# A two-layer gated network on one core: other places for projection steps, transform sums and gate steps in the queues

## The chip, the core and the metric

The kernel runs on one core of a Trainium2 chip. A core has five engines, each with a queue of its own that it works through in order: TensorE (PE; its weight loads are listed as PEld), VectorE (DVE), ScalarE (ACT), GpSimd (POOL) and SyncE (SP, which here only issues DMAs). Semaphores order the engines among each other. The metric is device time in microseconds, from the start to the end of one execution; lower is better. The profile gives the TensorE clock that was granted as a share of full speed: in this case it is 1.00 or 0.50 at any moment.

## The reference

Inputs are x and a context of 8 sequences of 256 tokens by 1024 features, all float32. Two layers follow one another; each adds a gated mixing step and a gated feed-forward step to x.

```
x = x + tanh(g_xattn[0]) * autocorrelation(layernorm(x), ctx, ctx)
x = x + tanh(g_ffn[0])   * lora_ffn(layernorm(x))
x = x + tanh(g_xattn[1]) * attention(layernorm(x), ctx, ctx, mask)
x = x + tanh(g_ffn[1])   * fourier_ffn(layernorm(x))
```

- autocorrelation: correlate x and the context along the sequence by Fourier transforms, per feature; keep the 11 largest lags of each feature, softmax over them, and add up the context shifted by those lags (positions past the end repeat the last token).
- lora_ffn: x W' + b, plus a low-rank product whose rank (8, 16, 32 or 64) the best of four gate scores selects for each token.
- attention: 32 query heads, 8 key and value heads of 128, with rotary positions; keys and values come from the context.
- fourier_ffn: a linear layer plus a low-rank update whose coefficients are masked and passed through a real Fourier basis. It is linear in x, so it can be folded into one matrix.

## The kernel before

**Passes and stages.** The batch is worked in two passes of four sequences. A pass has four stages: `autocorrelation`, `lora_ffn`, `attention`, `fourier_ffn`. x stays in SBUF as eight tiles of 128 rows by 1024 in each pass. The second half of each sequence is stored turned round, so that a transform along the sequence works on sums and differences of the two halves.

**Products by seven.** All large products are made with seven half-size products in place of eight (`SEVEN = (1, 2, 6, 7, 4, 5, 3)` is their order). `left_operands` and `right_operands` make the operands from four sums or differences of quarters. Which engine makes the sums is an argument. `combine` and `add_product` take the seven results out of PSUM.

**Stage 1.** `autocorrelation` runs beside a generator, `keys_values`, that makes the attention's keys and values of all tokens in the pass. One call of `fill(1)` draws one step from it: half of one of the seven products, eight matmuls of 256 columns (L794). A block of 512 tokens has four weight halves (two of keys, two of values) of 14 steps each, so 56 steps, and a pass has two blocks. In pass 0 the generator goes on with `fold_last_layer` (17 steps, L302 and L320), which makes the last stage's matrix and stores it in DRAM. In the first block of pass 0 the weight sums are made on the fly by `made_weight`: those of the keys on VectorE, those of the values (`wv`) on GpSimd, as eight instructions (L154, L158). Each block after the first makes four context sums as eight GpSimd instructions. The weights' loads are queued after the fourth product of the weight half before.

The autocorrelation works on half batches: one sequence by 512 features, eight in a pass. `turn(this, before, coming)` handles three of them at once:

1. for `coming`, it loads the context rows `cn` and the row `end`;
2. for `this`, it transforms the keys' sums (`ke`, `ko`; L412) and the queries' (`qe`, `qo`), copies spectra to SBUF on ACT, and multiplies them (`products`: four VectorE multiplications, then two GpSimd sums, L432 and L434 or L436). The results of the multiplication are `re` and `im`;
3. it transforms the values' half frequencies (`vr`, `vi`);
4. for `coming`, `sums` makes the normed rows `xn` on ACT (L453), then `ke`, `ko`, `qe`, `qo` on GpSimd (L461 to L464), and corrects `ke` on VectorE (L467);
5. for `before`, it transposes the weights of the lags (`both`; L515), transforms them, and multiplies with the keys' and values' spectra: `er`, `ei`, then `odr`, `odi`;
6. for `this`, `correlation` (L561, L562) returns `re` and `im` to lags, in two parts; `lags` finds the largest on VectorE and weighs them; GpSimd forms `both` from the result `w` (L552, L553). Between the parts `back(0)` and `back(1)` return the values of `before` in two matmuls each (L531), and `residual` (L371) adds them to x.

`fill` calls stand between these steps. When no `before` exists (the first half batch), those inside `if before` aren't made; a last turn has only a `before`.

At the start of a pass, `loads(order[0])`, two small tables and `late()` (the loads of six x tiles) are queued on SP, then `fill`, the norm of the first sequence, `sums` of the first half batch and another `fill`.

**Stages 2 and 4.** Both feed-forward stages work on four pairs of row tiles. `prepare` norms a tile, transposes it on PE (L366) and copies it back on ACT as `xnT`, which has two buffers. In `lora_ffn` it also computes the low-rank product and the gate scores (`pa`, L623) and forms the gated low-rank activations `xa` in a chain of small VectorE instructions (L630 to L642). `turned` transposes `xa` on PE (`px`, L647) and copies it on ACT (`xaT`); `neg` is its negative, for the fourth product. `left` makes the pair's operand sums. `project` runs the seven products of the pair before (L670 with L679, and L1123), with the results in four PSUM buffers, and yields after each in `lora_ffn`. The sums of the first pair are made on VectorE, those of the other three on GpSimd (L206 to L209).

**What sets the order.** The text gives each instruction its engine and a rank. The order in the engines' queues is laid out when the program is built and isn't always the order of the text: in the trace, transposes of the next stage stand among the fold's last matmuls. Within a queue the engine waits at the instruction in front.

Of the kernel before, what the change touches and what calls it, by code (L numbers as in the profile page):

```python
# [11 lines left out]
F32 = mybir.dt.float32  # L12
# [3 lines left out]
ALU = mybir.AluOpType  # L16
# [3 lines left out]
P = 128  # L20
# [9 lines left out]
R0 = 64  # L30
# [9 lines left out]
KH = KC // 2  # L40
# [6 lines left out]
def flamingo_kernel(ctx: ExitStack, tc: tile.TileContext, a: dict, out: bass.AP):  # L47
    nc = tc.nc
# [320 lines left out]
    def residual(xs, ps, g):  # L369

        nc.vector.scalar_tensor_tensor(xs, ps, g, xs, ALU.mult, ALU.add)  # L371
# [12 lines left out]
    def autocorrelation(p, xt, pools, beside, late):  # L384
        c1, w1, w2, ps_dft, ps_cor, ps_out = pools

        def fill(n):
            for _ in range(n):
                next(beside, None)
# [59 lines left out]
        def sums(b, cols, cn, end):  # L449

            xn = big_tile("xn", [2, HALF], "xn")
            for i, lin in enumerate(norms[b]):
                nc.scalar.activation(  # L453
                    xn[:, i, :],
                    xt[b * 2 + i][:, cols],
                    AF.Identity,
                    bias=lin[:, 1:2],
                    scale=lin[:, 0:1],
                )
            qe, qo, ke, ko = one("qe"), one("qo"), one("ke"), one("ko")  # L460
# [12 lines left out]
        def turn(this, before, coming):  # L473


            after = None
            if this:
                b, cols, end, qe, qo, ke, ko = this
                if coming:
                    coming = loads(coming)  # L480
                kr_ps, ki_ps = dft((KCE, ke)), dft((KSE, ko), (NYQ, ke))


                kr, ki, kn = sb("kr"), sb("ki"), sb("kn")
                nc.scalar.copy(kr, kr_ps)
                nc.scalar.copy(kn, kr_ps)
                nc.scalar.activation(ki, ki_ps, AF.Copy, scale=pair)
                nc.scalar.copy(kn[0:1, :], ki_ps[0:1, :])
                re, im = sb("re"), sb("im")
                products(spectrum((CE, SE), (qe, qo)), kr, ki, kn, re, im, False)  # L490
                fill(2)

            if this:
                vr_ps, vi_ps = dft((KCO, ko)), dft((KSO, ke))
                vr, vi = sb("vr"), sb("vi")
                nc.scalar.copy(vr, vr_ps)
                nc.scalar.copy(vi, vi_ps)

                nc.vector.scalar_tensor_tensor(
                    kr[0:1, :], end[0:1, :], 2.0 * S, kr[0:1, :], ALU.mult, ALU.add  # L500
                )
                if coming:
                    after = sums(*coming)
                fill(2)
            last = not this
            if before:
                if last:
                    fill(3)
# [12 lines left out]
                fill(2 if last else 1)  # L521
                odr, odi = one("odr"), one("odi")
                products(spectrum((CO, SO), wt[::-1]), bvr, bvi, bvr, odr, odi, True)
                fill(3 if last else 1)

            def back(l):

                if before:
                    po = ps_out.tile([P, HALF], F32, tag="out", name="po")
                    for i, (k, sp) in enumerate(((0, er), (3, odi)) if l == 0 else ((1, ei), (2, odr))):  # L530
                        nc.tensor.matmul(po, inv2[:, k, :], sp, start=(i == 0), stop=(i == 1))  # L531
                    residual(b_tiles[0][:, b_cols], po, tg_x[0])
                    residual(b_tiles[1][:, b_cols], po, ntg_x[0] if l else tg_x[0])
                    fill(1)

            if last:
                back(0)
                back(1)
                return None, None
            w = big_tile("xn", [4, S], "w")  # L540
            cor = correlation(re, im, 0)
            fill(1)
            back(0)
# [48 lines left out]
        nc.sync.dma_start(inv, a["dft_inv"])  # L592
        inv2 = c1.tile([P, 4, P], F32, name="inv2")
        nc.sync.dma_start(inv2, a["lag_inv"])
        late()
        fill(6 if p == 0 else 4)
        normalize(0, 1)
        this, before = sums(*first), None
        fill(7 if p == 0 else 3)
        for i in range(len(order)):  # L600
            this, before = turn(this, before, order[i + 1] if i + 1 < len(order) else None)
            if i == 0:
# [4 lines left out]
    def lora_ffn(xt, w0, make_w0, ag, bl, beside):  # L607

        with (
# [32 lines left out]
                    nc.vector.tensor_scalar(xa[:, r], pa[:, r], past[:, i : i + 1], None, ALU.mult)  # L642
                return xnT, xa

            def turned(xnT, xa):
                px = ps_s.tile([R0 + 1, P], F32, tag="s", name="px")
                nc.tensor.transpose(px, xa, ident)  # L647
                xaT = w2.tile([R0 + 1, P], F32, tag="xaT", name="xaT", bufs=4)
                nc.scalar.copy(xaT, px)
                return xnT, xaT  # L650

            def left(m, first, second):
                q = [[s[0][:, k * KH : (k + 1) * KH, :] for k in range(2)] for s in (first, second)]
                s = [w2.tile([P, KH, P], F32, tag=f"s{i}", name=f"s{i}") for i in (1, 2, 4)]
                ops = left_operands(nc.gpsimd if m else nc.vector, q, *s)
                neg = w2.tile([R0 + 1, P], F32, tag="neg", name="neg")
                nc.vector.tensor_scalar(neg, second[1], -1.0, None, ALU.mult)
                return ops, first[1], second[1], neg

            def project(m, ops, up, low, neg):  # L660
                x = [
# [27 lines left out]
            for m in range(TT // 2):  # L689
                norm = norm_stats(xt[m * 2 : m * 2 + 2])  # L690
                got = [prepare(m * 2 + i, norm) for i in range(2)]
                steps = project(*pending) if pending else iter(())
                for _ in range(2):
                    next(steps, None)
                got = left(m, *(turned(*x) for x in got))
                if pending is None and make_w0:
                    w0.update(make_w0())
                for _ in steps:
                    pass
                pending = (m, *got)  # L700
            beside(w2, ps_t, "t")
            for _ in project(*pending):
                pass
# [382 lines left out]
    def fourier_ffn(p, xt, groups):  # L1086
        with (
# [16 lines left out]
                transposed(xnT, xn, ps_t, "t")  # L1104
                return xnT

            def left(m, first, second):
                q = [[s[:, k * KH : (k + 1) * KH, :] for k in range(2)] for s in (first, second)]
                s = [w2.tile([P, KH, P], F32, tag=f"s{i}", name=f"s{i}") for i in (1, 2, 4)]
                return left_operands(nc.gpsimd if m else nc.vector, q, *s)  # L1110

            def project(m, ops):
                x = [
# [25 lines left out]

            pending = None  # L1140
            for m in range(TT // 2):
                got = left(m, prepare(m * 2), prepare(m * 2 + 1))
                if pending is not None:
                    project(*pending)
                pending = (m, got)
# [207 lines left out]
```

## Time and profile before

Three runs took 3439.76, 3440.97 and 3441.66 us, with 3440.97 as the median. The profiled execution took 3440.27; its span, from the first instruction to the last, is 3438.5.

| what | us |
| --- | --- |
| span | 3438.5 |
| PE busy | 3335.6 |
| DVE busy | 2227.5 |
| POOL busy | 1413.8 |
| ACT busy | 860.5 |
| PE waits longest at L531 for POOL's `odi` (8 times) | 18.1 |
| one step of the generator, L794, 8 matmuls (63.73 to 65.46) | 1.73 |
| GpSimd sum of 128 x 512 (L206, mean) | 1.27 |
| VectorE sum of 128 x 512 (L206, 436.80) | 0.68 |
| granted clock, mean | 0.984 |

Stage by stage in the first pass: the autocorrelation runs to about 403, the first feed-forward stage from there to about 560, attention to 1647 and the last stage to 1757. The second pass follows in the same order and ends at 3438.5.

How to read it: an engine that is busy all the time bounds the kernel; its idle time, and what ended each idle stretch, tell what could be gained. In a list of waits a row names the waiting engine, its tile and line, whom it waited for, the total in microseconds, how often, and the longest. In a timeline a row has the start, the duration, the engine, line, operation, output and inputs; brackets give the idle time just before it and what ended it. Where rows are merged, the number of instructions is given with x.

### The profile page before, as it was taken

The page shows a single profiled execution, that of the slowest core. Times are in us where ns is not written, and L with a number is a line of the kernel's source. Part 1 is how long each engine was busy: PE and PEld are TensorE (multiplying, and loading weights), DVE is VectorE, ACT ScalarE, POOL GpSimd, SP SyncE. Part 2 cuts the span into 40 slices and gives each one's busy share as a digit, 9 for nine tenths or more (in the row PEclk, how much of TensorE's full clock was granted, in tenths as well). Part 3 has the DMA queues.
Part 4 walks back from the last instruction along what each step waited for, and adds up shares of the span by engine and source line. Part 5 has one row for each costly group of instructions (what it writes and reads, how often), then busy time and mean ns, then how long its engine had stood idle before and what let it go on. Part 6 is the DMA issues. An engine that isn't in the chain of part 4 may idle for free. (4 is left out here: it accounts for less than half of the span.)

```text
span 3438.5 us, 36954 instructions
## 1 busy us (share of the span) xinstructions
PE 3335.6 (97%) x12784; PEld 2287.7 (67%) x12784; DVE 2227.5 (65%) x4181; ACT 860.5 (25%) x2061; POOL 1413.8 (41%) x1259
## 2 busy tenths in 40 slices
PE   7899989999999999999999999999999999999998
PEld 6576545877766776776466666477777776776754
DVE  7677555877777666666557675456666666666562
ACT  2232101222222322223123321122222322222220
POOL 3665222343443344344546542323443344344443
PEclk9899889999999999999999999999999999999999
DMA  7343533333333333343153334053333333333411
GB/s 266 117 141 108 189 144 128 127 137 135 135 135 125 121 117 124 119 160 112 62 193 116 135 114 148 0 178 114 119 123 116 117 119 123 120 117 126 156 38 49
DMA packets 161864, 431.72 MB, mean 126 GB/s; under 512 B 21476, under 2 KB 56292, under 8 KB 161678
## 3 DMA queue, kind: packets, MB, share of 16 engines
q1 hardware_dynamic: 160526, 425.17, 36.7%
q0 software_dynamic: 1152, 4.19, 0.3%
q8 instruction: 102, 1.67, 0.2%
q14 instruction: 84, 0.69, 0.1%
HBM read 350.66 MB, written 78.64 MB: 125 GB/s over the span
## 5 line engine op out<-in xcount | busy, mean ns | idle before, releaser
L715 POOL TENSOR_TENSOR qT<-rope,rope 128x512 f32<-128x512 f32 x128 | 170.1, 1329 | 864.9 <-DVE rope L714 864.9
L950 PE MATMUL po<-wo,oT 128*128 128x512 f32 x960 | 432.1, 593 | 0.0
L921 PE MATMUL ps_q<-xn,wq 128*128 128x256 f32 x1920 | 428.9, 379 | 0.0
L371 DVE SCALAR_TENSOR_TENSOR x<-po,tg,x 128x512 f32<-128x512 f32 x376 | 268.8, 745 | 227.1 <-PE po L950 70.6
L921 PEld LDWEIGHTS ps_q<-xn,wq 128*128 128x128 f32 x1920 | 365.0, 190 | 50.3 <-PE po L679 0.5
L983 ACT ACTIVATE s<-s,nmx 128x256 f32<-128x256 f32 x512 | 255.9, 500 | 275.1 <-DVE nmx L980 274.6
L978 DVE COPY_PREDICATED s<-keep,ps_s 128x512 f32<-128x512 uint8 x256 | 186.1, 730 | 182.4 <-PE ps_s L969 178.9
L950 PEld LDWEIGHTS po<-wo,oT 128*128 128x128 f32 x960 | 177.5, 190 | 175.5 <-issue 170.4
L950 PE MATMUL po<-wo,oS 128*128 128x512 f32 x640 | 287.7, 593 | 0.3 <-DVE x L371 0.3
L921 PE MATMUL ps_q<-xn_t,wq 128*128 128x256 f32 x1280 | 285.6, 379 | 0.0
L1010 ACT COPY wT<-pt 128x512 f32<-128x512 f32 x256 | 138.0, 590 | 516.3 <-PE pt L1004 516.3
L921 PEld LDWEIGHTS ps_q<-xn_t,wq 128*128 128x128 f32 x1280 | 243.3, 190 | 33.0
L1015 PE MATMUL av<-wT,v 128*128 128x256 f32 x1024 | 247.7, 385 | 2.9 <-ACT wT L1010 2.9
L969 PE MATMUL ps_s<-kT,qT 128*128 128x256 f32 x1024 | 248.1, 379 | 0.0
L1015 PEld LDWEIGHTS av<-wT,v 128*128 128x128 f32 x1024 | 192.4, 191 | 78.0 <-issue 43.9
L992 DVE TENSOR_SCALAR s<-s,tot 128x256 f32<-128x256 f32 x512 | 219.6, 469 | 7.7
L977 POOL MEMSET s<- 128x512 f32 x256 | 129.9, 527 | 223.0 <-PE pt L1004 221.3
L950 PEld LDWEIGHTS po<-wo,oS 128*128 128x128 f32 x640 | 119.0, 190 | 136.6 <-issue 128.9
L969 PEld LDWEIGHTS ps_s<-kT,qT 128*128 128x128 f32 x1024 | 192.0, 190 | 25.4 <-DVE x L371 0.5
L258 POOL TENSOR_TENSOR x<-x,part 128x512 f32<-128x512 f32 x80 | 114.8, 1435 | 196.4 <-ACT part L257 196.4
L980 DVE TENSOR_REDUCE nmx<-s 128x2 f32<-128x512 f32 x256 | 175.0, 685 | 8.3
L263 POOL TENSOR_TENSOR x<-x,part 128x512 f32<-128x512 f32 x80 | 102.9, 1287 | 166.9 <-DVE part L371 143.7
(259 smaller groups left out, 5643.1 us busy)
## 6 DMA issues: line engine op xcount, KB each, us to landing
wq<-in_wq_dram SPq DMA_DIRECT2D x104, 512.0 KB, 3.3
wo<-in_wo_dram SPq DMA_DIRECT2D x104, 512.0 KB, 3.4
wq<-wq_d SPq DMA_DIRECT2D x96, 512.0 KB, 3.2
wo<-wo_d SPq DMA_DIRECT2D x96, 512.0 KB, 3.2
w<-w_d SPq DMA_DIRECT2D x36, 512.0 KB, 4.5
wk<-in_wk_dram SPq DMA_DIRECT2D x26, 512.0 KB, 5.4
wv<-in_wv_dram SPq DMA_DIRECT2D x26, 512.0 KB, 4.1
wk<-wk_d SPq DMA_DIRECT2D x24, 512.0 KB, 3.8
```

What stands on the lines that cost most here:

```text
L371: nc.vector.scalar_tensor_tensor(xs, ps, g, xs, ALU.mult, ALU.add)
L715: nc.gpsimd.tensor_add(dst, t0, t1)
L921: nc.tensor.matmul(ps[:, l, :], wops[r][:, l, c, :], xo[r][:, c, :], start=(c == 0), stop=(c == KH - 1),)
L950: nc.tensor.matmul(po, ops[r][:, h, t * P : (t + 1) * P], wops[r][:, h, :], start=(h == 0), stop=(h == 1),)
L969: nc.tensor.matmul(ps[:, t, :], qT[i, n][:, l, t * P : (t + 1) * P], kT[:, n * S : (n + 1) * S], start=True, stop=True,)
L977: nc.gpsimd.memset(s, MASKED)
L978: nc.vector.copy_predicated(s, keep[b], ps)
L980: nc.vector.tensor_reduce(nmx, s, AX.X, ALU.max, negate=True)
L983: nc.scalar.activation(s[:, t, :], s[:, t, :], AF.Exp, bias=nmx[:, t : t + 1], accum_out=tot[:, t : t + 1],)
L992: nc.vector.tensor_scalar(s[:, t, :], s[:, t, :], tot[:, t : t + 1], None, ALU.mult)
L1010: nc.scalar.copy(wT[i], pt)
L1015: nc.tensor.matmul(av[:, i, :], kv[step][1][:, n * 2 + c, :], wT[i][:, c, :], start=(c == 0), stop=(c == 1),)
```

## The change

It changes five things.

1. `fill` counts in the autocorrelation. Before the first half batch, pass 0 draws 12 and 9 steps instead of 6 and 7, and pass 1 draws 0 and 7 instead of 4 and 3. The 12 are drawn ahead of `late()`, so the six x loads come behind what these steps queue. Inside a turn, the step count after the values' transforms goes from 2 to 6 in the first turn of pass 0, from 2 to 1 in its later turns, and stays 2 in pass 1. After the second products it goes from 1 to 2. The fill behind `back(1)` goes.
2. `sums(*coming)` is called after the products of `before` instead of ahead of them.
3. The two returns change places: the first takes `ei` and `odr`, the second `er` and `odi`; the signs follow.
4. In `lora_ffn`, `left` comes ahead of `turned`, and `turned` and `neg` come three products later.
5. All operand sums of both feed-forward stages are made on VectorE.

```diff
-                if coming:
-                    after = sums(*coming)
-                fill(2)
+                fill((1 if p == 0 else 2) if before else 6 if p == 0 else 2)
...
                 products(spectrum((CO, SO), wt[::-1]), bvr, bvi, bvr, odr, odi, True)
-                fill(3 if last else 1)
+                fill(3 if last else 2)
+            if this and coming:
+                after = sums(*coming)
...
-                    for i, (k, sp) in enumerate(((0, er), (3, odi)) if l == 0 else ((1, ei), (2, odr))):
+                    for i, (k, sp) in enumerate(((0, er), (3, odi)) if l else ((1, ei), (2, odr))):
                         nc.tensor.matmul(po, inv2[:, k, :], sp, start=(i == 0), stop=(i == 1))
                     residual(b_tiles[0][:, b_cols], po, tg_x[0])
-                    residual(b_tiles[1][:, b_cols], po, ntg_x[0] if l else tg_x[0])
-                    fill(1)
+                    residual(b_tiles[1][:, b_cols], po, tg_x[0] if l else ntg_x[0])
+                    fill(1 - l)
...
+        if p == 0:
+            fill(12)
         late()
-        fill(6 if p == 0 else 4)
         normalize(0, 1)
         this, before = sums(*first), None
-        fill(7 if p == 0 else 3)
+        fill(9 if p == 0 else 7)
...
-                got = left(m, *(turned(*x) for x in got))
+                ops = left(*(x[0] for x in got))
                 if pending is None and make_w0:
                     w0.update(make_w0())
+                for _ in range(3):
+                    next(steps, None)
+                up, low = (turned(x[1]) for x in got)
+                neg = w2.tile([R0 + 1, P], F32, tag="neg", name="neg")
+                nc.vector.tensor_scalar(neg, low, -1.0, None, ALU.mult)
                 for _ in steps:
                     pass
-                pending = (m, *got)
+                pending = m, ops, up, low, neg
...
-                return left_operands(nc.gpsimd if m else nc.vector, q, *s)
+                return left_operands(nc.vector, q, *s)
```

More of the change, by code (lines that the diff above doesn't have):

```diff
@@ L643, in prepare, with turned @@
                 return xnT, xa
-            def turned(xnT, xa):
+            def turned(xa):
                 px = ps_s.tile([R0 + 1, P], F32, tag="s", name="px")
@@ L649, in turned, with left @@
                 nc.scalar.copy(xaT, px)
-                return xnT, xaT
-            def left(m, first, second):
-                q = [[s[0][:, k * KH : (k + 1) * KH, :] for k in range(2)] for s in (first, second)]
+                return xaT
+            def left(first, second):
+                q = [[s[:, k * KH : (k + 1) * KH, :] for k in range(2)] for s in (first, second)]
                 s = [w2.tile([P, KH, P], F32, tag=f"s{i}", name=f"s{i}") for i in (1, 2, 4)]
[L655 to L658, printed above, removed]
+                return left_operands(nc.vector, q, *s)
             def project(m, ops, up, low, neg):
@@ L1105, in prepare, with left @@
                 return xnT
-            def left(m, first, second):
+            def left(first, second):
                 q = [[s[:, k * KH : (k + 1) * KH, :] for k in range(2)] for s in (first, second)]
                 s = [w2.tile([P, KH, P], F32, tag=f"s{i}", name=f"s{i}") for i in (1, 2, 4)]
-                return left_operands(nc.gpsimd if m else nc.vector, q, *s)
+                return left_operands(nc.vector, q, *s)
             def project(m, ops):
@@ L1141, in fourier_ffn @@
             for m in range(TT // 2):
-                got = left(m, prepare(m * 2), prepare(m * 2 + 1))
+                got = left(prepare(m * 2), prepare(m * 2 + 1))
                 if pending is not None:
```

## The prediction

> **What bounds the kernel now.** First the busy times and the clock row of the page:
>
> ```profile
> PE 3335.6 (97%) x12784; PEld 2287.7 (67%) x12784; DVE 2227.5 (65%) x4181; ACT 860.5 (25%) x2061; POOL 1413.8 (41%) x1259
> ...
> PEclk9899889999999999999999999999999999999999
> ```
>
> PE is busy for 97% of the span, and the change removes no matmul. So it can win only what PE idles (3438.5 - 3335.6 = 103 us, 5.9 of it before the first matmul and 9 behind the last) and what matmuls lose at half clock. Second, the waits of PE alone (total, times, longest):
>
> ```profile
> PE po L531 <- POOL odi L434: 18.1, 8, 5.4
> PE po L531 <- POOL re L432: 11.7, 4, 9.2
> PE px L647 <- DVE xa L642: 10.4, 6, 1.7
> ...
> PE ps_cor L561 <- POOL re L432: 5.7, 1, 5.7
> ...
> PE ps_cor L562 <- POOL im L436: 2.9, 1, 2.9
> ```
>
> These 48.8 us stand at places that the diff touches: L531 is the values' return, L561/L562 the correlation, px the turned gates. Third, stretches in time (us, busy time of PE, PEld, DVE, ACT, POOL, granted clock, DMA):
>
> ```profile
> 47.80:58.00 10.20, 6.30 (x14) 4.59 (x15) 9.77 (x15) 0.30 (x1) 9.67 (x7) 0.50 0.23 73
> 99.00:119.50 20.50, 8.21 (x15) 4.73 (x16) 16.80 (x37) 1.45 (x4) 13.37 (x10) 0.50 0.20 78
> 157.00:160.40 3.40, 3.40 (x8) 2.08 (x7) 1.74 (x3) 0.00 (x0) 3.28 (x3) 0.50 0.14 46
> ...
> 1942.20:1952.40 10.20, 7.83 (x14) 3.96 (x13) 8.08 (x24) 1.41 (x3) 5.04 (x4) 0.50 0.19 59
> ```
>
> Behind a wait the granted clock is 0.50, so half of the PE time in such a stretch is lost besides the wait. Fourth, what POOL does before the longest wait (PE stands from 96.7 to 105.9):
>
> ```profile
> 90.06 2.49 POOL L154 TENSOR_TENSOR wv_s<-wv,wv 128x512 f32<-128x512 f32 x2
> 92.52 2.48 POOL L158 TENSOR_TENSOR wv<-wv,wv 128x512 f32<-128x512 f32 x2
> ...
> 104.58 1.27 POOL L432 TENSOR_TENSOR re<-ma,mb 128x512 f32<-128x512 f32 x1
> ...
> 111.61 1.71 POOL L434 TENSOR_TENSOR odi<-ma,mb 128x512 f32<-128x512 f32 x1
> ```
>
> The values' weight sums (eight of about 1.24, 10 us) lie ahead of the parts that PE awaits, and u and c behind them hold DVE's rope, which idles 12.1 us. Fifth, the gates while POOL forms the next pair's sums:
>
> ```profile
> 476.29 1.94 DVE L634 TENSOR_TENSOR sc<-sc 128x1 f32<-128x1 f32 x2
> ...
> 478.26 1.31 DVE L636 TENSOR_SCALAR past<-sc,best 128x3 f32<-128x3 f32 x1
> ...
> 480.28 0.29 PE L647 MATMUL px<-ident,xa 128*65 128x128 f32 x1 [1.73 <-DVE xa L642]
> ```
>
> With POOL silent, one L634 takes 0.15 and L636 0.23 (497.5 to 499.1).
>
> **The change, part by part.** One call of the keys' and values' generator is eight matmuls, 1.73 us of PE.
>
> (a) More calls ahead. Pass 0 has drawn 14 when its first half batch starts and 20 at that turn's end; afterwards 22 and 32. Pass 1 keeps 8, with the norm queued ahead of them. In pass 0 the correlation's waits (5.68 + 2.89 = 8.57) lie at 43 to 53, when DVE and POOL make the products. The calls that should fill them need the second key weights, issued from 33.3 to 39.2 and landing 8.6 to 10.9 later, with DMA at 0.9 and more of its time. The six loads of x (3 MB, 7 us at 410 GB/s) are put behind these calls' DMAs: a store of k, four of weights, four loads, two stores of k, whose last is out at 43.9. If SP keeps that order, the weights land up to 7 us sooner; x lands by about 44 + 6 + 8 = 58, and the second half batch's cn goes out at 50 instead of 44. Their readers are the third half batch's xn (ACT, 79.1) and the second's transforms (68.9): 11 us or more hide both, and past that a late load costs its lateness. I take 6 of the 8.57 and 1 of the half clock's 3.15 (6.30 / 2): 7 us; bounds 0 (weights late) and 11.7.
>
> (b) The values' weight sums are made in call 29, which moves from the second turn into the first, where no values' return waits on POOL. Their waits, 9.24 + 5.39 = 14.63, and 8.21 / 2 = 4.1 of clock go. Late next is the second half batch's ke and ko, behind 10 us of sums: 10 + 2 x 1.27 against four calls and two correlations of PE work (6.9 + 3.5 = 10.4), 2 us, and with u and c in between 5; with its clock I charge 7.7. That leaves 11 of 18.7; bounds 0 and 18.7.
>
> (c) Values' parts and next sums. The first return now takes ei and odr instead of er and odi: odr is out 1.25 before odi. One more call stands ahead of it (1.73): 2.98 more slack. The waits there are 2.09 and 0.39 + 2.56 in pass 0, and 1.40, 1.58, 0.70 + 1.67, 1.36 + 2.58, 0.85 in pass 1: 15.2 us, of which 2.98 leaves only 0.96. The next half batch's four sums (4 x 1.27 on POOL, two 0.76 on ACT, one 0.68 on DVE) no longer come ahead of er to odi. Half clock behind those waits: 3.4 / 2 twice, 7.83 / 2, 3.4 / 2: 9.0. The stretch at 1942 also follows a 1.9 us wait for DVE that stays. I take 14.2 + 5.3 = 19.5; bounds 8 (a third) and 24.2.
>
> The Trainium skill (TensorE: Matmul & The Clock Gate, "Why this matters for your kernels") says that idle gaps up to about 3 us don't bring the half clock back. The stretch at 157.0 follows a wait of 2.09 and has 0.50, so here the measurement decides. By the rule this part would give 14.2 instead of 19.5.
>
> (d) Sums queued later. The cost is on the next turn's first transform. In the turn at 206 to 244 odi ends at 232.1; four sums after it end at 237.2, ke's DVE step at 238; the transform starts at 243.8: 6 us of slack. In the turns where POOL also makes the context's sums (eight, 10 us) 4 us are missing; that is one turn in each pass, with half of it in clock. Charge 4; bounds 0 and 14 (1 us in each of 14 turns).
>
> (e) Gates and sums of the first FFN. Six waits of 1.73. Their cause is DVE slowed beside POOL's L206 to L209, which go to DVE (4 x 0.68 instead of 4 x 1.27); the turn is asked three products later (10 us). The second gate can't come sooner, since its tile is written only when the pair before has read the buffer, in its fifth product. neg waits on DVE for ACT's 0.26 us copy of the turned gates, with evictions 3.4 us apart behind it, so it holds no one. I take 10; bounds 0 (DVE sums queued into the chain keep it as late) and 10.4.
>
> (f) Sums on VectorE in both FFNs: 12 groups of 2.7 us, or 7 where POOL runs beside them (L154 on DVE took 1.77 at 52.9 instead of 0.68). Behind them in the queue stand the evictions that free PSUM for PE. The cover is a pair's PE time, 34.9 and 25.8 us with DVE about half busy, and four PSUM buffers of 3.4 each. Cost 0; without cover 12 x 2.7 = 33.
>
> (g) Four calls of the fold move into the last turn. The stretch from 409.6 to 447.1 at 0.50 (37.1 busy) stays: 0, bounds -5 and +5.
>
> Sum: 7 + 11 + 19.5 - 4 + 10 = 43.5. The profiled execution took 3440.3, 1.8 around its span of 3438.5; 3440.3 - 43.5 = 3396.8. The median of the runs is 0.7 higher, so 3397.5, rounded to **3397**.
>
> **Rivals.**
>
> 1. *The POOL waits change places.* (a) and (b) together give 4 and (d) takes 8: 4 + 19.5 - 8 + 10 = 25.5, 3416. For it: POOL's work stays the same, only its order moves. Against: the first turn has no return for it to delay.
>
> 2. *All of it goes*: 11.7 + 18.7 + 24.2 + 10.4 = 65 and none of (d): 3376. For it: the queues have slack in most turns (no wait from 180 to 270). Against: 10 us blocks remain on POOL.
>
> 3. *Slower: the next sums land behind this half batch's "both".* POOL waits there for ACT's w (102.3 us in 14 waits, 15.6 the longest). At 213.0 both is done; sums behind it would end ke and ko at 215.5 and DVE at 216.2, against a transform at 205.9: 10.3 a turn. It decides from five of the 14 turns on (43.5 / 10.3); in eight it is 82 - 43.5, 3480. For it: sums now stand directly ahead of both. Against: their inputs are loaded a turn's length before.
>
> 4. *Short waits don't lower the clock*, and the half-rate stretches behind waits under 3 us stay: 5.3 less, 3402. For it: the wait of 3.02 at 306 is followed by full clock; against, 157.0. This is the Trainium skill's rule above.
>
> 5. *The change doesn't do what it says*, since queue order isn't text order: the fold's masks are loaded at 80.8, 300 us before their use, and the next stage's transposes run among the fold's matmuls. Then x keeps its place, the calls fill as before, and (c)'s swap and (e) remain: 8 + 10, 3423.
>
> **How the numbers follow.** Forecast 0.42; rivals 0.20, 0.15, 0.08, 0.06, 0.09. What a measurement can tell from no change is 0.2%, 7 us: 3434 to 3448. Faster holds all but rival 3 and the ends of 1 and 5: 0.86; same 0.05; slower 0.09. The range runs from 3373, under rival 2, to 3432, over rival 5, and leaves out rival 3 and the far ends of (d) and (f). The forecast's own range is 3385 to 3408.
>
> **What would show it.** (a): no wait at L561/L562 before 60 us. (b): L154/L158 of wv run on POOL before the first "both", and no wait over 6 us in 60 to 120. (c): L531 waits under 4 us in all, and now for odr. (d): waits of L412 on ke or qe. (e): no px wait, and L634 at 0.15. (f): no wait of L670 or L1123 for DVE evictions. I am wrong if L412 shows more than 20 us of waits, or if PE's idle time falls by less than 20.

## The result and the profile after

The changed kernel takes 3409.8 us (median of six executions, 3400.7 to 3412.6), beside 3440.4 for the kernel before (3438.8 to 3445.2). The ratio is 0.9907, with a 95% interval from 0.9894 to 0.9919. So it is 30.6 us faster; the forecast was 3397 with a range from 3373 to 3432. The median lies in the range, 13 us above the forecast and just outside the narrower range, 3385 to 3408, that the prediction gave for its main line.

The profiled execution is the fastest of the six: 3400.7, span 3399.0. Where half-clock stretches fall differs from one execution to the next, so a single profile of this kernel may be 9 us from its median.

In the lines of the changed kernel, L531 has become L532, L561/L562 are L562/L563, L647 is L649, L634/L636 are L636/L638 and L794 is L798; L428 to L467 keep their numbers. From its page, the busy times and the clock:

```profile
PE 3319.6 (98%) x12784; PEld 2281.0 (67%) x12784; DVE 2245.2 (66%) x4229; ACT 859.5 (25%) x2061; POOL 1355.3 (40%) x1211
...
PEclk9999899999999999999999999999999999999999
```

The number of matmuls is the same. What PE does not work is 3399.0 - 3319.6 = 79.4 us, 23.5 less than the 102.9 before; its busy time is 16.0 less; the mean granted clock is 0.989 instead of 0.984. Together that is the 39.5 between the two profiled spans. The kernel turn_early below has the same instructions in the same order, and its profile (3409.2) lies near the median: there PE is without work for 26.1 us less than before and busy for 5.0 less, 31.1 together. So by that profile the greater part of what was won is waits, and little of it is clock.

The waits of PE in the changed kernel (total, times, longest) at the places that the prediction named:

```profile
PE po L532 <- DVE x L371: 5.9, 4, 4.0
...
PE dft L412 <- DVE ke L467: 5.4, 1, 5.4
...
PE po L532 <- POOL odr L432: 3.9, 1, 3.9
...
PE po L532 <- DVE neg L576: 3.7, 1, 3.7
...
PE ps_k L798 <- DVE wk_s L158: 3.4, 1, 3.4
PE po L532 <- POOL im L434: 2.0, 2, 1.2
...
PE px L649 <- DVE xa L644: 0.8, 1, 0.8
```

The waits of the correlation (8.6 us) are gone, and so are the two long ones of the return behind the values' weight sums (14.6) and nearly all of px (10.4). But the other waits at the return, 15.2 us before, are 15.5 now (5.9 + 3.9 + 3.7 + 2.0; 13.6 in turn_early), only with other releasers. That is the term that failed.

Two waits that the prediction did not name are gone as well. These are rows of the kernel before, where PE waits for weights of the first FFN and for VectorE's sum of them:

```profile
452.36 3.70 PE L670 MATMUL po<-w,xnT 128*128 128x512 f32 x8 [3.60 <-DMA w<-in_w_dram]
...
462.56 3.70 PE L670 MATMUL po<-w_t,s 128*128 128x512 f32 x8 [2.89 <-DVE w_t L140]
```

Together they are 6.5 us. In the kernel before, six of these eight loads are issued between 446 and 450, after the first product has begun at 443; in the changed kernel all eight are issued between 417 and 423, and the first product begins at 425.

The stretches that correspond to those of the prediction, by time (PE, PEld, DVE, ACT, POOL, granted clock, DMA):

```profile
44.00:54.00 10.00, 6.63 (x32) 5.54 (x31) 9.91 (x15) 0.00 (x0) 2.24 (x2) 1.00 0.91 334
84.00:104.50 20.50, 15.14 (x48) 9.28 (x47) 18.36 (x54) 9.06 (x17) 11.10 (x8) 0.83 0.65 195
...
1947.00:1966.00 19.00, 13.66 (x37) 7.70 (x37) 17.34 (x41) 5.69 (x11) 7.55 (x7) 0.82 0.34 105
```

The first had 0.50 and now 1.00. The second had 8.21 of PE work in 20.5 us at 0.50, now 15.14 at 0.83. The third, in the second pass, still has a lowered clock. From the timeline, the values' weight sums and what follows them:

```profile
73.12 2.94 POOL L154 TENSOR_TENSOR wv_s<-wv,wv 128x512 f32<-128x512 f32 x2
76.02 3.39 POOL L158 TENSOR_TENSOR wv<-wv,wv 128x512 f32<-128x512 f32 x2
...
86.42 1.70 POOL L461 TENSOR_TENSOR ke<-cn 128x512 f32<-128x512 f32 x1
```

```profile
89.94 2.08 PE L412 MATMUL dft<-ke,mats 128*128 128x512 f32 x2 [5.36 <-DVE ke L467]
```

They run 17 us earlier than before (at 73 instead of 90), ahead of the first "both", and POOL comes to ke only behind them: the transform waits 5.36 for it. Last, the gates of the first FFN, for the second tile of the second pair:

```profile
451.18 0.15 DVE L636 TENSOR_TENSOR sc<-sc 128x1 f32<-128x1 f32 x1
...
452.58 0.22 DVE L638 TENSOR_SCALAR past<-sc,best 128x3 f32<-128x3 f32 x1
```

One step on a column takes 0.15 again, where two took 1.94 beside POOL.

### The profile page after: what moved, and what is told of

Read it like the earlier page. It is cut to its first block, busy times and chain, and to the rows that moved or that the text cites. A ratio compares the mean times of both kernels' runs of the same rounds, so it can differ in the third digit from the quotient of the medians.

```text
span 3399.0 us, 36938 instructions
## 1 busy us (share of the span) xinstructions
PE 3319.6 (98%) x12784; PEld 2281.0 (67%) x12784; DVE 2245.2 (66%) x4229; ACT 859.5 (25%) x2061; POOL 1355.3 (40%) x1211
## 5 line engine op out<-in xcount | busy, mean ns | idle before, releaser
L371 DVE SCALAR_TENSOR_TENSOR x<-po,tg,x 128x512 f32<-128x512 f32 x376 | 269.0, 745 | 201.3 <-PE po L954 70.6
L258 POOL TENSOR_TENSOR x<-x,part 128x512 f32<-128x512 f32 x80 | 114.9, 1436 | 213.5 <-ACT part L257 193.6
L716 DVE TENSOR_TENSOR rope<-c,tab_q 128x512 f32<-128x512 f32 x128 | 88.4, 691 | 125.8 <-POOL c L240 119.9
```

## The experiments

Each experiment stands with what was expected of it before it ran; A and B are the two theories of that text. There are twelve kernels, in the order in which they follow here. The times are medians (fastest to slowest), each with its ratio to the kernel before on the same chip (3442 to 3443 there).

| run | what differs from the changed kernel | us | ratio, 95% interval |
|---|---|---|---|
| turn_early | gates turned three products earlier | 3410.2 (3405.2 to 3411.2) | 0.9900 (0.9885 to 0.9915) |
| pool_sums | FFN sums on GpSimd again | 3421.3 (3419.5 to 3423.8) | 0.9937 (0.9923 to 0.9950) |
| x_loads_first | x loads ahead of the 12 steps | 3412.5 (3405.3 to 3415.0) | 0.9906 (0.9893 to 0.9920) |
| fills_only | numbers of calls and place of x loads alone | 3426.3 (3420.0 to 3428.5) | 0.9954 (0.9940 to 0.9967) |
| sums_early | next sums at their old place | 3415.3 (3413.8 to 3421.7) | 0.9922 (0.9908 to 0.9935) |
| returns_old | values' parts in their old places | 3409.3 (3408.1 to 3410.0) | 0.9904 (0.9889 to 0.9920) |
| two_out_banks | returns 2 banks, transforms 3 | 3434.0 (3432.3 to 3436.4) | 0.9973 (0.9962 to 0.9984) |
| second_return_own_bank | second return in a transforms' bank | 3416.2 (3414.6 to 3417.5) | 0.9924 (0.9910 to 0.9937) |
| sums_behind_returns | next sums behind both returns | 3406.5 (3402.1 to 3410.4) | 0.9898 (0.9882 to 0.9915) |
| q_sums_on_vector | qe, qo on VectorE | 3405.7 (3403.9 to 3411.9) | 0.9896 (0.9880 to 0.9913) |
| call_sums_on_vector | u, c of a call on VectorE | 3395.6 (3391.8 to 3398.0) | 0.9861 (0.9846 to 0.9877) |
| call_sums_and_ke_on_vector | u, c and ke on VectorE | 3381.0 (3376.5 to 3387.0) | 0.9816 (0.9802 to 0.9829) |

### The gates: later turn, or sums on VectorE?

turn_early takes the three products out again:

```diff
-                for _ in range(3):
-                    next(steps, None)
                 up, low = (turned(x[1]) for x in got)
```

> The changed kernel, with the turned gates asked three products earlier again; the sums stay on VectorE. Theory A (the px waits came from VectorE's gate chain running slowly beside GpSimd's sums, so taking these sums off GpSimd removed them): px waits stay under 2 us in all, time as the changed kernel, 3400 to 3413. Theory B (asking three products later removed them): six waits of about 1.7 us come back, 10 us more, about 3420.

pool_sums puts the sums of pairs 2 to 4 back on GpSimd and leaves the later turn:

```diff
-            def left(first, second):
+            def left(m, first, second):
...
-                return left_operands(nc.vector, q, *s)
+                return left_operands(nc.gpsimd if m else nc.vector, q, *s)
...
-                ops = left(*(x[0] for x in got))
+                ops = left(m, *(x[0] for x in got))
```

The last stage gets the same edit.

> The changed kernel, with the operand sums of pairs 2 to 4 in both feed-forward stages on GpSimd again; the gates stay late. Theory A (port shared by VectorE and GpSimd slows the gate chain): six px waits of 1.7 us come back, L636 near 1 us instead of 0.15, 10 us slower than the changed kernel, about 3419. Theory B (the later turn removed the waits): px waits stay under 2 us, time within 3 us of the changed kernel.

The first measured 3410.2, and the order of the instructions on every engine is that of the changed kernel: where the turn stands in the text changes nothing in the queues. So it is also a second set of executions of the changed kernel. The second measured 3421.3, and its waits of PE show px again (seven waits, 10.9 us):

```profile
PE px L649 <- DVE xa L644: 10.9, 7, 1.7
```

Both are as theory A had them. What wins here is the sums' engine alone, worth 11.5 us (3421.3 - 3409.8).

### The first 60 us: the place of the x loads

x_loads_first:

```diff
-        if p == 0:
-            fill(12)
         late()
+        if p == 0:
+            fill(12)
```

> The changed kernel, with the six x loads queued ahead of the 12 steps again; all step counts as changed. Theory A (the loads' place decides whether the second key weights come early enough to fill the first half batch): PE's waits at L562/L563 for POOL come back, 6 to 9 us before 60 us, and with the clock 6 to 12 us are lost, about 3419. Theory B (the step counts decide): no wait there, time within 3 us of the changed kernel.

It measured 3412.5. Its waits of PE:

```profile
PE ps_v L798 <- DVE c L244: 5.3, 1, 5.3
...
PE ps_cor L562 <- POOL re L432: 4.9, 1, 4.9
...
PE ps_cor L563 <- POOL im L436: 2.9, 1, 2.9
```

The correlation waits again as before the change, so it is the x loads' place that lets the calls fill that hole: with them first the second key weights land by 46.6, in the changed kernel by 39.0. But the wait of 5.36 for ke, the one of 3.4 for VectorE's sum of the second key weights (L158) and one of 0.4 beside it are gone, and one of 5.3 has come. The median is within 3 us of the changed kernel's: theory A was right about the waits, B about the time.

### What the transforms' part is worth, edit by edit

fills_only is the kernel before with the diff's numbers of `fill` calls and the place of `late()`; parts, sums and FFNs are the old ones.

> The kernel before with the change's numbers of calls and the place of the x loads alone: parts and sums in their old places, the FFNs as before. The run with sums on GpSimd again had all of the transforms' part and took 3421.3. Theory A (of the transforms' part the calls carry it, the swap and the late sums bring nothing): 3417 to 3426. Theory B (swap and late sums bring some 10 of it): 3429 to 3436. By the prediction's terms, with (c) at 19.5 and (d) at -4, it would be 3437.

sums_early:

```diff
                 )
+                if coming:
+                    after = sums(*coming)
                 fill((1 if p == 0 else 2) if before else 6 if p == 0 else 2)
...
-            if this and coming:
-                after = sums(*coming)
```

> The changed kernel with the next half batch's sums asked at their old place, ahead of both products; POOL gets qe and qo earlier, by several instructions. Theory A (what the later sums gave POOL was lost at the bank, so their place is worth little): L532 waits 12 to 22, the sum of L412 waits not over 8, time 3406 to 3418. Theory B (the later sums hold all that part (c) still brought, and the first return waits for POOL again): L532 waits over 24, most for POOL odr or odi, time 3420 to 3428.

returns_old:

```diff
-                    for i, (k, sp) in enumerate(((0, er), (3, odi)) if l else ((1, ei), (2, odr))):
+                    for i, (k, sp) in enumerate(((0, er), (3, odi)) if l == 0 else ((1, ei), (2, odr))):
...
-                    residual(b_tiles[1][:, b_cols], po, tg_x[0] if l else ntg_x[0])
+                    residual(b_tiles[1][:, b_cols], po, ntg_x[0] if l else tg_x[0])
```

> The changed kernel with the values' parts in their old places (er and odi first, ei and odr second). POOL, ACT and SP keep their queues; only the returns on PE and their residuals' signs change places. Theory A (the swap gives the first return 1.25 of slack, but the bank's release for the second return is no earlier, so a wait before the first return is a wait not taken at the second): L532 waits 15 to 19 in all, time 3408 to 3416. Theory B (the swap is worth its 1.25 at most of the 14 first returns, as the prediction had it): L532 waits of 24 or more, most of them for POOL odi, time 3420 or more.

fills_only measured 3426.3, some 16 us under the kernel before and between its two theories. In it the correlation's waits, the two long ones of the return and the two for the first FFN's weights are gone, and the other waits at the return are 20.0 us. pool_sums has the whole change of the transforms with the FFNs' sums as before, so swap and late sums together are worth 3426.3 - 3421.3 = 5 us; the two intervals overlap. sums_early measured 3415.3, five more than the changed kernel. Its waits at L532 (13.6 us) hardly differ, and those of the calls (L798, for VectorE) are longer, 31.3 us instead of 13.9: A was right about the return, and the time lies in A's bounds. The wait of 5.36 for ke is in neither fills_only nor sums_early: with the sums at their old place POOL forms ke at 77 to 78, between the weight sums, and not behind them. returns_old measured 3409.3: the swap is worth nothing that these runs can tell. Its waits of PE:

```profile
PE po L532 <- POOL odi L434: 19.6, 6, 6.4
...
PE po L532 <- DVE neg L576: 3.0, 1, 3.0
```

At 22.6 us the waits at L532 are over A's 15 to 19 and near B's 24, yet the time is A's: with this order they are longer there, and the calls behind wait less (the waits at L798 for DVE are 9.5 instead of 13.9). What does not come earlier is the whole, not the one part that is asked last.

### Is the one PSUM bank the hold?

Returns and turned lag weights share one bank. two_out_banks gives them two and the transforms three of their four:

```diff
-            tc.tile_pool(name="ac_dft", bufs=4, space=PSUM) as ps_dft,
+            tc.tile_pool(name="ac_dft", bufs=3, space=PSUM) as ps_dft,
...
-            tc.tile_pool(name="ac_out", bufs=1, space=PSUM) as ps_out,
+            tc.tile_pool(name="ac_out", bufs=2, space=PSUM) as ps_out,
```

> The changed kernel, with two PSUM banks for the returns and the transposed lag weights, and three instead of four for the transforms. Theory A (the second return waits because the one bank is freed by residuals that stand late in VectorE's queue): waits of L532 for VectorE, 9.6 us in the changed kernel, fall under 2, and 5 to 10 us are won, about 3402. Theory B (the returns are late because VectorE is late with the products, whatever the bank): L532 waits stay near 15 us in all, and three transform banks add waits at L412, 3410 to 3425.

second_return_own_bank leaves the four and takes the second return's tile from them; every queue keeps its order:

```diff
-                    po = ps_out.tile([P, HALF], F32, tag="out", name="po")
+                    po = (ps_dft if l else ps_out).tile([P, HALF], F32, tag="dft" if l else "out", name="po")
```

> The changed kernel, but the second return's tile is taken from the transforms' four PSUM banks instead of the one bank that it shares with the first return. Every engine's queue keeps its order. Theory A (the waits of the return have only changed places: they are now the second return's, which waits until the first return's residuals on VectorE have freed the one bank): the L532 waits that end with DVE (5.9 + 3.7 in the changed kernel's profile) fall below 2, L412 gains less than 3, and the time falls by 8 to 12, to 3398 to 3402. Theory B (as with two banks for the returns and three for the transforms, the waits only move on to the transforms): L412 waits rise above 10 and the time is 3410 or more.

They measured 3434.0 and 3416.2, both slower than the changed kernel, and the first slower than either theory had it. The L532 waits fall to 1.4 and to 4.1 us. The waits of PE, first in two_out_banks, then in second_return_own_bank:

```profile
PE dft L412 <- ACT kn L486: 19.8, 6, 4.7
PE dft L412 <- DVE ma L430: 18.3, 6, 6.8
```

```profile
PE dft L412 <- DVE x L371: 10.4, 3, 5.2
```

The second is the clear one. The residual (x, L371), for which the second return waited, now holds up the transforms of the next half batch, three times and longer in all. So theory A fell: the bank decides only which instruction waits. What it waits for is VectorE, which is late. Why it is late was the question for the rest.

### What makes VectorE late?

In the changed kernel POOL runs qe and qo between odr and odi in four of the 14 turns. sums_behind_returns asks for the sums behind `back(1)`, which puts qe and qo behind odi everywhere; q_sums_on_vector makes them on VectorE:

```diff
-            nc.gpsimd.tensor_add(qe, xn[:, 0, :], xn[:, 1, :])
-            nc.gpsimd.tensor_sub(qo, xn[:, 0, :], xn[:, 1, :])
+            nc.vector.tensor_add(qe, xn[:, 0, :], xn[:, 1, :])
+            nc.vector.tensor_sub(qo, xn[:, 0, :], xn[:, 1, :])
```

> The changed kernel with the next half batch's sums asked behind the second return instead of ahead of the correlation. In the changed kernel POOL runs qe and qo between odr and odi in four of the 14 turns, the ones in which L532 waits longest; here they stand behind odi in every turn. Theory A (those two instructions, 2.6 to 3.4 us on POOL and slowing VectorE's rope beside them, are what keeps the return late): L532 waits fall from 15.7 to under 8, no wait over 3 for DVE x, time 3400 to 3405. Theory B (POOL's total work is what holds, and qe and qo come late for the next transforms instead): L412 waits rise by 5 or more, or L532 waits stay over 12, time 3408 or more.

> The changed kernel with qe and qo formed on VectorE instead of GpSimd, 16 times two instructions of 512 columns (0.69 each alone). Theory A (the return is late since POOL's blocks of instructions both come late and slow VectorE beside them): POOL 40 us less busy, L532 waits under 8, time 3398 to 3405. Theory B (VectorE is the late engine by its own load, and 1.4 more of it per turn makes residuals and products later): L532 or L412 waits on DVE rise to 15 or more, time 3412 or more.

They measured 3406.5 and 3405.7, both within the changed kernel's own spread and between the times of their two theories. In the first the waits of the return fall to 10.2, not under A's 8, and new ones come for qe, as its theory B had it:

```profile
PE dft L412 <- POOL qe L463: 6.2, 2, 3.8
```

In the second they stay at 16.5, where A had under 8. So these two sums are not it either. The list of VectorE's own waits in the changed kernel, for the second pass's transforms (1740 to 2060), tells more:

```profile
DVE ke L467 <- POOL ke L461: 27.3, 7, 8.0
...
DVE rope L716 <- POOL c L240: 11.4, 3, 6.5
...
DVE v L244 <- POOL u L238: 3.6, 1, 3.6
```

Here VectorE waits for POOL, with the products and the residuals behind it in its queue. The first pass has 26.0, 5.6 and 4.0 of the same (90 to 330). The last two kernels take these waits away, by forming the inputs on VectorE itself:

```diff
-    def combine(r, ps, tiles, new, dest):
+    def combine(r, ps, tiles, new, dest, eng=nc.gpsimd):
...
-            nc.gpsimd.tensor_add(tiles["u"], tiles["u"], m)
+            eng.tensor_add(tiles["u"], tiles["u"], m)
...
-            nc.gpsimd.tensor_add(c, tiles["w"], m)
+            eng.tensor_add(c, tiles["w"], m)
...
-                done = combine(r, ps, tiles, new, dest)
+                done = combine(r, ps, tiles, new, dest, nc.vector)
```

> The changed kernel with the generator's own u and c (L238, L240) formed on VectorE instead of GpSimd in the calls for keys and values; PE's queue keeps its order. In the changed kernel's profile a key's rope (L716) stands on VectorE ahead of the products of odr and odi and waits there for POOL's c: 5.6 in the first pass, 11.4 in the second, and v (L244) 7.6 for POOL's u. Theory A (it is this wait at the head of VectorE's queue that makes the returns late, whatever their order and whatever bank): VectorE's waits for L238 and L240 go (24.6 us), L532 waits fall from 15.7 to under 8 and the time by 6 to 12, to 3398 to 3404. Theory B (VectorE's own work holds, 0.69 more for each of the two per call): the residuals come as late, L532 or L798 waits for DVE of 15 or more, time 3409 or more.

```diff
-            nc.gpsimd.tensor_add(ke, cn[:, 0, :], cn[:, 1, :])
+            nc.vector.tensor_add(ke, cn[:, 0, :], cn[:, 1, :])
```

> As before, and ke (L461) is formed on VectorE too, so that L467 need not wait for POOL (26.0 and 27.3 us of VectorE's waits in the changed kernel's two passes). Theory A: VectorE's waits for POOL's ke go as well, the wait of 5.4 of the transform for ke at 84.6 with them, L532 waits under 6; 4 to 10 faster than with u and c alone, 3390 to 3398. Theory B (ke's wait lies in VectorE's slack): no change against u and c alone, within 3 of it.

The first edit is made in the calls for keys and values only; the second kernel has both edits. They measured 3395.6 and 3381.0, and neither's slowest execution reaches the changed kernel's fastest (3400.7). With u and c alone VectorE's waits for them are gone from these stages, but the L532 waits are 15.7, so that count of theory A failed, and its time was better than A's: PE's time without work is 75.3 instead of 79.4 and its busy time 2.2 less, against a profile of the changed kernel that was its fastest execution. With ke as well VectorE has no waits for ke, u or c left in the transforms' stages. Of that kernel, the page's busy times and the waits of PE:

```profile
PE 3321.2 (98%) x12784; PEld 2284.1 (67%) x12784; DVE 2293.6 (68%) x4277; ACT 861.2 (25%) x2061; POOL 1310.3 (39%) x1163
```

```profile
PE po L532 <- DVE x L371: 6.4, 3, 2.5
...
PE po L532 <- POOL odr L432: 3.6, 2, 2.3
```

PE is without work for 3385.3 - 3321.2 = 64.1 us, L412 waits no longer, and the return waits 10.0 instead of 15.5. VectorE is 48 us busier than in the changed kernel, and the kernel is 28.8 us faster: it is 1.8% under the kernel before (0.9802 to 0.9829) and the best of all that ran. ke without u and c was not tried, so how much each brings by itself is known for u and c only.

VectorE does reach the products sooner. First in the changed kernel, then in this one, it is there before PE's transform this often:

```profile
DVE ma L428 <- PE dft L412: 20.5, 10, 8.2
```

```profile
DVE ma L428 <- PE dft L412: 29.9, 17, 8.2
```

But theory A's count for the return (under 6) failed again, and the time is better than A's 3390 to 3398. Of the 15.3 us less without work, 5.4 is the transform's wait for ke and 5.5 the return. The two edits also take 45 us of work off POOL. Less work on POOL does not by itself explain the gain: q_sums_on_vector takes 35 off it and wins nothing that shows. So it is shown that forming these three inputs on VectorE is worth 28.8 us and removes a third of the return's waits; what holds the other 10.0 is not shown.

## Why the prediction was right or wrong

**What bounds the kernel.** Right: what was won is PE's time without work and half clock, 26.1 and 5.0 us in turn_early's profile. Edit by edit the runs give 16 for the calls, 5 for swap and late sums and 11.5 for the first FFN's gates and sums; the prediction had 18, 15.5 and 10. The 13 us that the forecast is off lie in the second.

**(a) and (b).** The mechanisms were right. Taken together they were booked at 18, and the kernel with the numbers of calls alone won 16, but that they come so near is in part luck: these 16 hold the 6.5 us of the first FFN's weights, which no term had, and against them stand waits that no term had either, 3.3 for VectorE's sum of the second key weights, 3.7 at the start of the first FFN and 4.8 more at the return. The danger that (a) named, late weights, did not come: they land by 39.0, and no wait of PE is put down to their load; what is late is VectorE's sum of them. In (b) the weight sums stand where it put them. The late ke, 5.36 where (b) had said 2 to 5, comes from the sums' new place, which is (d)'s edit.

**(c), the step that failed.** "2.98 more slack ... 15.2 us, of which 2.98 leaves only 0.96", and from that 19.5. Measured: 15.5 us of waits remain at the return. The changed kernel's swap is worth nothing (returns_old), and swap and late sums together are worth 5, where (c) and (d) together had 15.5; from the profile before to the one after, the waits only change their releaser.

One premise of the step did not come about: that the next half batch's four sums "no longer come ahead of er to odi". The text of the kernel asks for them later, but in POOL's queue only qe and qo moved. The changed kernel, one turn (re is er here):

```profile
145.54 1.26 POOL L461 TENSOR_TENSOR ke<-cn 128x512 f32<-128x512 f32 x1
150.79 1.27 POOL L432 TENSOR_TENSOR re<-ma,mb 128x512 f32<-128x512 f32 x1 [3.99 <-DVE mb L429]
...
154.47 1.28 POOL L434 TENSOR_TENSOR odi<-ma,mb 128x512 f32<-128x512 f32 x1
155.70 1.28 POOL L463 TENSOR_TENSOR qe<-xn 128x512 f32<-128x512 f32 x1
```

So it is in all twelve turns that have both a half batch before and one to come: ke and ko stand ahead of er, as in the kernel before, and VectorE's step on ke (L467) ahead of the products.

The step also took each wait as its releaser's place in POOL's queue, so that a part asked later, or one with fewer sums ahead of it, would come free. The row of 1.9 us that the prediction set aside as "a wait for DVE that stays" leads to what was late there. The kernel before, around that place, in the timeline:

```profile
1932.17 2.52 POOL L158 TENSOR_TENSOR cx_t<-cx,cx_t 128x512 f32<-128x512 f32 x2
...
1932.28 7.86 DVE L467 SCALAR_TENSOR_TENSOR ke<-end,ke 128x512 f32<-128x512 f32 x1 [10.75 <-POOL ke L461]
...
1937.07 2.52 POOL L158 TENSOR_TENSOR cx_t<-cx_t,cx 128x512 f32<-128x512 f32 x2
...
1940.67 0.67 DVE L428 TENSOR_TENSOR ma<-dft,kr 128x512 f32<-128x512 f32 x1
...
1943.97 2.08 PE L531 MATMUL po<-re,inv 128*128 128x512 f32 x2 [0.70 <-POOL re L432]
```

VectorE stands 10.75 us for POOL's ke, an input of the next half batch, then takes 7.86 over it, and only then starts the products of the half batch before. PE's first transform for these products is done at 1931.2, so here it is the 7.86 that makes them late: the first starts at 1940.67. All four parts are late with it, so which of them is asked first matters little. In two other turns whose returns wait (at 272 and at 1865) it is the wait for ke itself: VectorE's step on ke ends 4.3 us after PE's first transform for the products. The list puts the return's wait down to POOL (re, odi), which came last, but POOL itself waited for VectorE's products. The same place in the changed kernel:

```profile
1948.21 1.33 POOL L432 TENSOR_TENSOR odr<-ma,mb 128x512 f32<-128x512 f32 x1
...
1948.78 5.05 DVE L716 TENSOR_TENSOR rope<-c,tab 128x512 f32<-128x512 f32 x1
...
1951.97 1.31 POOL L434 TENSOR_TENSOR odi<-ma,mb 128x512 f32<-128x512 f32 x1
...
1953.85 0.69 DVE L717 TENSOR_TENSOR rope<-c,tab 64x512 f32<-64x512 f32 x1
...
1958.47 0.73 DVE L371 SCALAR_TENSOR_TENSOR x<-po,tg,x 128x512 f32<-128x512 f32 x1
...
1959.92 2.07 PE L532 MATMUL po<-re,inv 128*128 128x512 f32 x2 [4.03 <-DVE x L371]
```

The first return has its parts at 1949.5 as planned. Its residual stands behind a rope of 5.05 and the lags and starts at 1958.47; the second return waits 4.03 for it.

**(d).** It was charged 4 for a late ke or qe. The one wait of L412 that came is the 5.36, which (b) had counted; elsewhere ke and ko were not moved, and the later sums are worth 5 on balance instead of costing. Had they been put later still, the cost named there would have come: 6.2 us of waits for qe in sums_behind_returns.

**(e).** 10 was right (10.4 of waits became 0.8, and the edit alone is worth 11.5). Of its two reasons, the slowed VectorE is shown; "the turn is asked three products later" is not a reason, since the queues are the same without it.

**(f) and (g).** No evictions hold PE up. (g) was put at 0; with the fold's calls made earlier the first FFN's weights come in time, the 6.5 us above, and fills_only has that too. The fold's half-rate stretch was 27.3 us in this profile instead of 37.5, 5 us won, and 37.6 in turn_early with the same queues: it is not the change's doing.

**The rivals.** Rival 1 (3416) came nearest in time: waits did change places, but mostly at the return and not in (a) and (b). Rival 2 fell with (c). Rival 3 needed sums behind "both", which the queue does not have. Rival 5 had two true parts: the text's order is not the queue's for `turned`, nor for ke and ko. Of rival 4 the runs say that neither side holds throughout. A wait of 2.19 of the changed kernel at 2049.5 left the clock at 1.00, the one of 2.09 before halved it; the rule of the Trainium skill (TensorE: Matmul & The Clock Gate, "Why this matters for your kernels") agrees with the one and not with the other.

## What to carry to other kernels

When the same engine is named at the end of several waits, look at what that engine itself waited for, and go on until an engine stands for its own work: here the list of PE named POOL, POOL waited for VectorE's products, and these stood in VectorE's queue behind a step on POOL's sum of the next half batch. And before counting on a new place in the text, look where the instruction stands in the engine's queue. An instruction that waits at the head of an in-order queue is paid by all behind it, so it can be cheaper to do its small input on the same engine, even the busier one. Before counting on a swap, ask who waits next for the buffer that is freed.

## What the runs showed of the hardware

**VectorE can be held for as long as GpSimd runs without a pause.** L467 and L716 normally take 0.69. The 7.86 us of L467 above end at 1940.14; POOL's six instructions in a row, with no gap, end at 1939.59. The 5.05 of L716 end at 1953.83, POOL's row at 1953.28. Twice more (3.95 at 1909.0 in the changed kernel, 4.47 at 1938.9 in the best one) the end is 0.55 behind the end of POOL's row too, and so it is with the longest of all, 10.29 at 1913.1 in sums_early. In other places the same instructions take 1.7 beside POOL. The Trainium skill (GPSIMD Engine Reference, "1. Specifications") says that GpSimd shares its SBUF interfaces with VectorE and that instructions of VectorE with two SBUF inputs contend; these rows agree, and the size of the hold is from them. What decides between 1.7 and a full hold stays open.

**The clock at the end of the transforms.** From the windows of the changed kernel, then of turn_early, which has the same queues:

```profile
398.40:425.70 27.30, 23.57 (x56) 12.70 (x55) 19.80 (x50) 2.90 (x5) 0.00 (x0) 0.50 0.80 289
```

```profile
393.40:431.00 37.60, 33.87 (x81) 18.56 (x81) 24.68 (x60) 4.07 (x7) 0.00 (x0) 0.50 0.72 260
```

PE has work for all but 3.7 us of either, much of it matmuls with 40 output rows (acc), and the granted clock is half all the same, for 27 us in one execution and 38 in another. No run here told why.
